# O's splits moved to block 1, VectorE's order in block 0's FFN changed, the overflow flag read earlier, and a tail whose down projection runs five steps back

## The chip, the cores and the metric

One core of a Trainium2 chip. The metric is the device time of one execution in microseconds (us). The kernel before takes 905.08 us (median of three runs, 904.69 to 905.27). The engines are named as in the profile: PE (TensorE, matmuls), PEld (its weight loads), DVE (VectorE), ACT (ScalarE), POOL (GpSimd) and SP (SyncE, which issues most DMAs).

## The reference, cut to what matters

x is 4 sequences of 1024 tokens with 512 features, in float32. A retention layer and a feed-forward network (FFN) stand each between two layer norms:

```python
x = x + _layernorm(attn(_layernorm(x)))      # attn, per token and feature:
#   q, v = x @ Wq.T, x @ Wv.T
#   ret[t] = lam * ret[t-1] + v[t]            (a scan along the sequence; 16 heads, one lam each)
#   out = layernorm(q * ret, gamma, beta) * silu(x @ Wg.T);  out @ Wo.T
x = x + _layernorm(ffn(_layernorm(x)))       # ffn:
#   silu(x @ fp8(gate_w) * gate_s) * (x @ fp8(up_w) * up_s) @ fp8(down_w) * down_s
```

The FFN is 512 to 1536 to 512, and its weights are rounded to 8-bit floats first.

## The kernel before, in words

**Blocks.** The 4096 tokens are NB = 8 blocks of TB = 512 tokens, each of NS = 4 sub-tiles of 128 tokens. The loop `for t in range(NB)` runs the FFN of block t in NI = 12 steps of 128 hidden features (`f.gate(i)`, `f.up(i)`, `f.fuse(i)`, `f.down(i - f.lag)`), and into its steps it weaves the retention layer of block t + 1 (object `b`), the first norm of block t + 2 (`n`) and the end of the FFN of block t − 1 (`l`). Block 0's retention layer, the splitting and rounding of weights, and block 1's v, q and g run ahead of the loop. `InOrder` keeps every engine's instructions in the order in which the code issues them; so an operation that waits holds up all behind it on its engine.

**Three passes.** From block FAST = 2 on (`fast`), and for block 1's v, q, g, a product in float32 is made of three passes on operands of fewer mantissa bits: top x top, low, and diff (`pass_of`, `o_pass`). `begin` makes the first two and then lets ACT scale the bank by 1 + LOW; `end` makes the diff pass and whatever reads the bank (scan for v, the product y for q with POOL's sum of y, SiLU for g). Activations are split by DVE: `cut_x` and `low_of` (an integer TENSOR_SCALAR, then a subtraction), `part_x` and `diff_of`.

**The splitter.** `Splitter` (line 323) does the same to weights. `units` numbers them: v is 0 to 3, q 4 to 7, g 8 to 11, o 12 to 15. `copy` ("c") copies a weight's chunk to DRAM, `split` ("s", line 365) is three DVE operations and one ACT scaling of 128x512, `store` ("k") writes parts to DRAM, and `keep` ("w") loads O's parts into `wo_parts`, which stays in SBUF. The table `times` (line 406) says at which block, step and place of the step O's are done, and `splitter.at(t, i, place)` does them. From block 2 on SP streams the parts of v, q, g and O's diff from DRAM into `w_ring`, four slots of 256 KB (`fetch_weights`).

**Rounding of the FFN's weights.** `round_weights` (line 175) takes 18 pieces; each is a DVE cast to 8 bits, a DMA of the next raw piece into the freed place, and an ACT copy back to SBUF, which also sums the piece into `over`. The generator yields three times a piece, and `rounds(n)` advances it n times. `pass_over` (line 200) makes one number of `over`: not zero if a weight overflowed. It writes a column of 128 numbers to DRAM, reads it back as a row, reduces it and writes `flag`. At the end every engine loads `flag`, and the program branches to a second, exact version if it isn't zero (label `beyond`).

**Block 0's FFN** (conditions `t == 0`) carries block 1's means and variances: `b.halves` splits a sum into two parts (ACT, then DVE), `b.mean` and `b.var` are two PE matmuls each with those parts, `center_y` subtracts, `z` scales and gates y, `o`, `o_moments`, `x1_of`, `x1n_of` finish the retention layer. It also carries block 2's first norm: `n.stats`, `rstd`, `shift`, `norm_x`, `send_x`, `low_of`, `diff_of`. Two PSUM banks with the tag `pf` serve gate and up in turn: gate's bank is freed by ACT's SiLU, up's by DVE's `fuse`.

**The tail** (from line 1493). In the last block the down projection lags by `self.lag` = 4 steps behind up, so 5 steps are left after the last up, done sub-tile by sub-tile. Then for each sub-tile DVE scales the bank (`scale`), makes statistics, ACT takes a root, DVE inverts it, the norm and the addition of x1 follow (`norm`, `add`), and a DMA writes `out`. The last sub-tile's addition is cut into two halves with a DMA each (`add_halves`).

Of the kernel before, what the change touches and what calls it, by code (L numbers as in the profile page):

```python
# [10 lines left out]
F32 = mybir.dt.float32  # L11
# [4 lines left out]
ALU = mybir.AluOpType  # L16

P = 128
# [5 lines left out]
def sandwich(  # L24
# [20 lines left out]
    nc = tc.nc  # L45
    NT, D = x.shape
# [3 lines left out]
    TB = 512  # L50
    NS = TB // P
    NB = NT // TB
# [7 lines left out]
    work = ctx.enter_context(tc.tile_pool(name="work", bufs=2))  # L60
# [6 lines left out]
    class InOrder:  # L67
# [9 lines left out]
    pe, dve, act, pool, sp = (  # L77
        InOrder(e) for e in (nc.tensor, nc.vector, nc.scalar, nc.gpsimd, nc.sync)
    )
# [116 lines left out]
    def rounds(n):  # L196
        for _ in range(n):
            next(rounding, None)
# [117 lines left out]
    operands = {}  # L316
# [4 lines left out]
    wo_parts = {}  # L321

    class Splitter:
# [40 lines left out]

        def split(self, n):
            k, c = units[n]
            if k == "o" and c == 0:
                w, top, low = wo_sb[:, c], self.room[0], self.room[1]
                diff = top
            elif k == "o" and c == 1:  # L370
                w = wo_sb[:, c]
                top = work.tile([P, D], F32, tag="rstd", name=f"top_o{c}", bufs=1)
                low = work.tile([P, D], F32, tag="ret", name=f"low_o{c}")
                diff = top
            elif k == "o":
                w, top = wo_parts["top"].bitcast(F32)[:, c], self.room[n % 2]
                low, diff = wo_parts["low"][:, c], top
            else:
                w, top = self.raw[k].bitcast(F32)[:, :, ts(c, P)], self.by_chunk(self.room[n % 2])
                low, diff = self.slot_of[k, c] = self.slots[len(self.slot_of) % len(self.slots)]  # L380
            dve.tensor_scalar(top.bitcast(I32), w.bitcast(I32), TOP_MASK, None, ALU.bitwise_and)
            dve.tensor_tensor(low, w, top, ALU.subtract)
            m = low.bitcast(F32)
            dve.scalar_tensor_tensor(diff, top, -LOW, m, ALU.mult, ALU.add)
            act.activation(low, m, AF.Copy, scale=1.0 / LOW)
            self.at_work[n] = {"diff": diff} if k == "o" and c > 1 else {"diff": diff, "low": low}

        def store(self, n):
            k, c = units[n]
# [11 lines left out]
        def keep(self, n):  # L401
            k, c = units[n]
            if c == 0:
                room = big.tile([P, 2, NC, D], F32R, tag="x1n0", name="wo_parts")
                wo_parts["top"], wo_parts["low"] = room[:, 0], room[:, 1]
            for part in ("top", "low"):
                if part in operands[k, c]:
                    sp.dma_start(wo_parts[part].bitcast(F32)[:, c], operands[k, c][part])

        times = {  # L410
# [4 lines left out]
        }  # L415

        def at(self, *when):
# [491 lines left out]
    class Ffn:  # L909
# [3 lines left out]
        def __init__(self, a):  # L913
            self.t, self.kept = a.t, a.kept
            self.parts = [a.x1nT[:, 0], a.x1nT[:, 1]]
            self.f, self.g = {}, {}
            self.last = self.t == NB - 1
            self.lag = 4 if self.last else 2
            self.x1, self.d = [], [None] * NS
            if self.last:  # L920
                self.more = [
                    big.tile([P, 2, 2, TB], F32R, tag=tag, name=f"more_{tag}") for tag in ("xnT", "y")
                ]
# [83 lines left out]
            center(self.d[s], self.d[s], self.mv[:, s, :])  # L1007

        def add(self, s, engine=pool):
            if engine is dve and s == NS - 1:  # L1010
                return self.add_halves(s)
            engine.tensor_tensor(self.d[s], self.d[s], self.x1[s], ALU.add)
            self.store(s)

        def add_halves(self, s):
            for h, queue in enumerate((sp, act)):
                cols = ts(h, D // 2)
                dve.tensor_tensor(self.d[s][:, cols], self.d[s][:, cols], self.x1[s][:, cols], ALU.add)
                queue.dma_start(out[ds(self.t * TB + s * P, P), cols], self.d[s][:, cols])

        def store(self, s):
            sp.dma_start(out[ds(self.t * TB + s * P, P), :], self.d[s])
# [11 lines left out]
    b = Retention(1)  # L1034
# [9 lines left out]
    a = Retention(0, x_first)  # L1044
    a.new_xnT()
    warm(14)
    early, later = slice(0, TB // Q // 2), slice(TB // Q // 2, TB // Q)
# [24 lines left out]
    wo_sb = load_square(woT, "wo_sb")  # L1072
# [27 lines left out]
    b.turn_x(1, "pd1")  # L1100
    a.v(3, "pf")
    a.scan(3)
    splitter.load("v")
    for n in range(2, 4):
        load_piece(n)
# [25 lines left out]
    a.var()  # L1131
    for s in range(NS):
        b.part_x(s)
    a.rstd_y()
    splitter.store(0)
    for c, home in enumerate(("pa0", "pf", "pf", "pa1")):
# [22 lines left out]
    a.o(2, "pd2")  # L1159
    rounds(3)  # L1160
    splitter.split(4)
    a.o_moments(2)
    a.x1_moments(1)
    a.x1_of(2)
    a.x1n_of(1)
    splitter.store(3)
    a.o(3, "pd3")
    a.new_x1nT()
    b.begin("v", 0, "pf")
    a.turn_x1n(0)  # L1170
    a.upper_of(0)
    a.o_moments(3)
    a.x1_moments(2)
    a.x1_of(3)
    a.x1n_of(2)
    a.rest_of(0)
    b.begin("v", 1, "pf")
    a.turn_x1n(1)
    a.upper_of(1)
    b.end("v", 0)  # L1180
    splitter.split(5)
    splitter.store(4)
    b.begin("v", 2, "pd0")
    a.rest_of(1)
    b.end("v", 1)
    a.turn_x1n(2)
    a.upper_of(2)
    b.begin("v", 3, "pd1")
    a.x1_moments(3)
    a.x1n_of(3)  # L1190
    a.rest_of(2)
    b.end("v", 2)
    splitter.split(6)
    splitter.store(5)
    b.begin("q", 0, "pd2")
    b.end("v", 3)
    b.begin("q", 1, "pd3")
    a.turn_x1n(3)
# [4 lines left out]
    a.rest_of(3)  # L1203
    b.begin("q", 2, "pf")
    b.end("q", 1)
    b.begin("q", 3, "pf")
    b.end("q", 2)
    rounds(3)
    b.end("q", 3)
    splitter.store(7)  # L1210
    rounds(3)

    l = None
    for t in range(NB):
        f, n = Ffn(a), None
        fast = b is not None and b.fast
        for i in range(NI):
            if t > 0 and (t > 1 or i) and not (fast and i == 11):
                (f if i else l).rest((i - 1) % NI)
            if t == 0 and i == 0:  # L1220
                n = Retention(2)

            if t > 0 and b and i == 0 and t < NB - 2:
                n = Retention(t + 2)
# [17 lines left out]
            if fast and i == 3:  # L1242
                l.stats(3)
                l.rstd()
                l.shift()
            if t == 0 and i == 4:
                b.z(0)
            if t == 0 and 7 <= i < 10:
                b.x1_moments(i - 7)
            f.gate(i)  # L1250
            if t == 0 and i in (5, 6):
                n.norm_x(2 * i - 10, True)
                n.norm_x(2 * i - 9, True)
# [22 lines left out]
            if fast and i == 6:  # L1276
                b.gate_y(3)
                b.cut_y(3)
            if t == 0 and i == 1:
                b.halves()  # L1280
            if t == 0 and i == 3:
                b.var()
            if t == 0 and i == 4:
                b.z(1)
            if t == 0 and i == 5:
                b.z(2)
                b.z(3)
            if t == 0 and 6 <= i < 10:
                b.o(i - 6)
            if t == 0 and i == 8:  # L1290
# [26 lines left out]
            if t == 0 and i == 1:  # L1317
                b.mean()
                b.center_y()
            if t == 0 and i == 2:  # L1320
                b.halves()
            if t == 0 and i == 9:
                load = b.move_x1n(2)
                load()
# [12 lines left out]
            if fast and i == 11:  # L1337
                for s in range(2):
                    b.upper_of(s)
                    b.rest_of(s)  # L1340
            if t == 0 and i == 3:
                b.rstd_y()
            if fast and i == 4:
                b.halves()
            if fast and i < 6:
# [23 lines left out]
            if fast and i == 7:  # L1369
                b.rest_of_y()  # L1370
            splitter.at(t, i, "mid")
            if t == NB - 1 and 1 < i < 5:
                next(passing, None)
            if n and t and i == 2:
                l.fetch(0, 2)
# [17 lines left out]
                    n.diff_of(2)  # L1393
                    n.diff_of(3)
            if t == 0:
                rounds(3 if 0 < i < 6 else 6 if i < 8 else 0)
                if i < 11:
                    f.rest(i)
                if 0 < i < 5:
                    n.stats(i - 1)  # L1400
                if i == 4:
                    n.rstd()
                    n.shift()
                if i == 8:
                    n.low_of(0)
                    n.low_of(1)
                if i in (9, 10):
                    n.low_of(i - 7)

            if l and not b and i in (4, 5):  # L1410
                l.stats(2 * i - 8)
# [91 lines left out]
    for s in range(2, NS):  # L1503
        for i in steps:
            l.down(i, [s])
    beyond = None
    if flag is not None:
        loads, (beyond,) = nc.values_load_multi_w_load_instructions(
            flag, min_val=0, max_val=0x7F800000,
            skip_runtime_bounds_check_because="it is compared with zero alone",  # L1510
        )
        for load in loads:
            tc.keep_in_program_order(load)
        tc.mark_branch_hint_location("beyond", beyond, engines=mybir.ALL_ENGINES)
    for s in range(NS):
        l.scale(s)
        l.stats(s)
        l.root(s)
        if s:
            l.add(s - 1, dve)  # L1520
        l.inverse(s)
        l.norm(s, shift_scale if s < NS - 1 else center_scale)
    l.add(NS - 1, dve)
    return beyond


# [92 lines left out]
```

## Time and profile before

| | |
|---|---|
| median of the runs | 905.08 us |
| the profiled execution | 904.03 us |
| its span | 902.2 us |
| instructions | 12010 |
| busy: PE, DVE, ACT, POOL | 881.1, 629.8, 419.0, 238.9 us |
| O splits on DVE, start | 148.91, 158.64, 197.31, 199.75 us |
| first gate matmul of block 0, of block 1 | 104.44, 192.87 us |
| last matmul's end | 892.65 us |
| landing of the last output | 900.01 us |

The profile is of one execution, whose own time stands in the table beside its span; sums over its rows are compared with it, and not with the median. All operations are issued through one helper line (L75), so groups are told apart by the tiles that they write and read: `pfg` and `pfu` are the banks of gate and up, `pd` that of down, `pv`, `pq`, `pg` those of v, q, g, `po` that of O; `mu` and `var` those of block 1's mean and variance; `half` the parts of a sum, `ysum` and `sqsum` POOL's sums; `split_room` and `wo_parts` the O splits; `scr` the rounding pieces. A row of waits says which engine's work on which tile ended the wait of another engine's instruction. The matmuls' listed durations overlap, so the distance of their starts is of more use than their lengths.

### The profile page before, as it was taken

The numbers are of one execution on the slowest core, as the hardware profiler recorded it, in microseconds if no ns is written. First come the engines' busy times: TensorE is split into PE (matmuls) and PEld (weight loads), VectorE is DVE, ScalarE is ACT, GpSimd is POOL, SyncE is SP. The second block draws the span as 40 slices with busy tenths as digits, with TensorE's granted clock in tenths as the row PEclk, the third lists the DMA queues.
The fourth block names the chain that finished last, engine by engine and source line by source line (L and its number), as shares of the span: only waits on it lengthen the run. The fifth ranks groups of instructions, "written<-read, shape, count | busy, mean of one in ns | idle before, by whom it ended". The sixth has DMA issues, their size and how long they took to land. (4 is left out here: it accounts for less than half of the span.)

```text
span 902.2 us, 12010 instructions
## 1 busy us (share of the span) xinstructions
PE 881.1 (98%) x3948; PEld 738.6 (82%) x3948; DVE 629.8 (70%) x1071; ACT 419.0 (46%) x741; POOL 238.9 (26%) x304
## 2 busy tenths in 40 slices
PE   9999999889999999999999999999999999999995
PEld 7465777678888888888888888888888888888885
DVE  4898788677587766876668675876758756665545
ACT  1358566533645336453464435553364523644323
POOL 1215212201415024230423214141232403322020
PEclk9999999999999999999999999999999999999998
DMA  9974444767563674646754766728746565424021
GB/s 284 304 217 157 151 171 157 205 234 237 171 176 96 232 237 136 153 153 204 250 149 97 232 205 193 187 58 258 226 148 152 154 197 149 152 73 117 0 94 50
DMA packets 116154, 153.73 MB, mean 170 GB/s; under 512 B 10931, under 2 KB 54708, under 8 KB 116020
## 3 DMA queue, kind: packets, MB, share of 16 engines
q1 hardware_dynamic: 115220, 152.23, 55.1%
q8 instruction: 33, 0.54, 0.2%
q10 hardware_dynamic: 864, 0.66, 0.2%
q14 instruction: 37, 0.30, 0.1%
HBM read 117.98 MB, written 39.06 MB: 174 GB/s over the span
## 5 line engine op out<-in xcount | busy, mean ns | idle before, releaser
L75 PE MATMUL pfg<-x1nT,gate_sb 128*128 128x512 f32 x768 | 182.8, 381 | 3.3 <-ACT gate L75 3.2
L75 PE MATMUL pfu<-x1nT,up_sb 128*128 128x512 f32 x768 | 183.2, 381 | 0.8 <-DVE gate L75 0.8
L75 PE MATMUL pd<-down_sb,fuse 128*128 128x512 f32 x720 | 170.5, 379 | 0.0
L75 PEld LDWEIGHTS pfg<-x1nT,gate_sb 128*128 128x128 f32 x768 | 144.2, 189 | 26.7 <-ACT gate L75 6.2
L75 PEld LDWEIGHTS pfu<-x1nT,up_sb 128*128 128x128 f32 x768 | 145.0, 189 | 23.6 <-issue 1.7
L75 PEld LDWEIGHTS pd<-down_sb,fuse 128*128 128x128 f32 x720 | 141.4, 197 | 14.5
L75 DVE SCALAR_TENSOR_TENSOR gate<-pfu,us_sb,gate 128x512 f32<-128x512 f32 x96 | 71.8, 747 | 67.0 <-PE pfu L75 54.8
L75 ACT CAST fuse<-gate 128x512 fp32r<-128x512 f32 x90 | 55.6, 617 | 126.9 <-DVE gate L75 125.2
L75 ACT ACTIVATE gate<-pfg,gs_sb 128x512 f32<-128x512 f32 x96 | 65.6, 683 | 95.5 <-PE pfg L75 95.4
L75 POOL TENSOR_SCALAR mv<-mv 128x1 f32<-128x1 f32 (+1 forms) x82 | 22.8, 278 | 315.0 <-DVE mv L75 312.9
L75 DVE TENSOR_TENSOR fuse<-gate,fuse 128x512 fp32r<-128x512 f32 x90 | 71.7, 797 | 7.4 <-ACT fuse L75 7.3
L75 POOL TENSOR_TENSOR d<-d,x 128x512 f32<-128x512 f32 x28 | 41.7, 1510 | 84.5 <-ACT d L75 70.6
L75 DVE BATCH_NORM_STATS2 st<-x 128x6 f32<-128x512 f32 x64 | 43.6, 681 | 15.2 <-POOL x L75 12.5
L75 POOL TENSOR_TENSOR mv<-mv,nhalf 128x1 f32<-128x1 f32 (+1 forms) x75 | 51.8, 691 | 6.2
L75 POOL TENSOR_TENSOR x<-x,x1n 128x512 f32<-128x512 f32 x32 | 44.7, 1403 | 23.4 <-ACT x1n L75 15.0
L75 ACT ACTIVATE pv<-pv 128x512 f32<-128x512 f32 x28 | 16.3, 581 | 52.9 <-PE pv L75 52.9
L75 POOL TENSOR_TENSOR sqsum<-sqsum,sq 128x512 f32<-128x512 f32 x24 | 33.6, 1401 | 16.0 <-ACT sq L75 8.7
L75 POOL TENSOR_TENSOR ysum<-y 128x512 f32<-128x512 f32 x8 | 10.2, 1275 | 104.2 <-DVE y L75 104.2
L75 DVE TENSOR_TENSOR y<-pq,y 128x512 f32<-128x512 f32 x28 | 19.1, 682 | 22.5 <-PE pq L75 22.5
L75 DVE SCALAR_TENSOR_TENSOR y<-y,lnb_sb,mids 128x512 f32<-128x512 f32 x28 | 27.0, 965 | 7.1 <-ACT mids L75 7.0
L75 ACT ACT_TABLE_LOAD x19 | 24.4, 1283 | 15.5 <-DVE var L75 11.1
L75 DVE BATCH_NORM_STATS2 st<-po 128x6 f32<-128x512 f32 x32 | 21.9, 683 | 13.4 <-PE po L75 13.4
(222 smaller groups left out, 1482.8 us busy)
## 6 DMA issues: line engine op xcount, KB each, us to landing
x<-in_x SPq DMA_DIRECT2D x52, 256.0 KB, 5.6
kept<-x SPq DMA_DIRECT2D x32, 256.0 KB, 2.9
x<-kept SPq DMA_DIRECT2D x32, 256.0 KB, 4.4
out<-d SPq DMA_DIRECT2D x31, 256.0 KB, 2.0
w_ring<-dtop_v SPq DMA_DIRECT2D x24, 256.0 KB, 4.1
w_ring<-dlow_v SPq DMA_DIRECT2D x24, 256.0 KB, 3.2
w_ring<-ddiff_v SPq DMA_DIRECT2D x24, 256.0 KB, 3.6
w_ring<-dtop_q SPq DMA_DIRECT2D x24, 256.0 KB, 2.6
```

The lines of the kernel that those rows point to most:

```text
L75: return lambda *args, **kwargs: tc.keep_in_program_order(op(*args, **kwargs))
```

## The change

1. **O's splits.** `split` treats all four chunks of O alike: the source is `wo_parts["top"]` (loaded at block 0's last step), the low part stays in `wo_parts`, and only diff is written to DRAM. `keep` loads top alone. The splits of O's chunks 0 and 1 leave block 0, and all four stand at the start of steps 2, 3, 4 and 5 of block 1.
2. **Ahead of the FFN.** Two `rounds(3)` are added, one behind `a.scan(3)` and one ahead of `a.rstd_y()`; others are spread differently. `a.o(3)` and block 1's v passes begin earlier, and the transposes and moments around them are reordered.
3. **Block 0's FFN.** `b.halves` comes ahead of `f.up`, `b.var` behind `f.fuse(3)`; the statistics of block 2's input come in two pairs (steps 2 and 3); `z` and `rstd_y` are placed differently; `n.low_of` comes up to a step earlier; the rounding's steps per FFN step change.
4. **The flag.** `pass_over` moves from block 7 to block 3, steps 0 to 2. ACT, SP and POOL also load the flag and get a branch hint in block 6, step 5; at the end all five engines load it, and only DVE and PE get the hint there.
5. **The tail.** `self.lag` is 5 in the last block, so 6 steps of down are left after the last up, 12 matmuls for each sub-tile instead of 10. The last sub-tile is centered ahead of its reciprocal, and then scaled and added in two halves of 256 columns, each one DVE operation and a DMA.

The diff's core:

```diff
-            if k == "o" and c == 0:
-                w, top, low = wo_sb[:, c], self.room[0], self.room[1]
...
+            if k == "o":
                 w, top = wo_parts["top"].bitcast(F32)[:, c], self.room[n % 2]
                 low, diff = wo_parts["low"][:, c], top
...
-            self.at_work[n] = {"diff": diff} if k == "o" and c > 1 else {"diff": diff, "low": low}
+            self.at_work[n] = {"diff": diff} if k == "o" else {"diff": diff, "low": low}
...
-            for part in ("top", "low"):
-                if part in operands[k, c]:
-                    sp.dma_start(wo_parts[part].bitcast(F32)[:, c], operands[k, c][part])
+            sp.dma_start(wo_parts["top"].bitcast(F32)[:, c], operands[k, c]["top"])
...
-            (0, 6, "end"): "s12", (0, 7, "start"): "k12", (0, 7, "end"): "s13", (0, 8, "start"): "k13",
-            (0, 11, "mid"): "w12 w13 w14 w15", (1, 0, "start"): "r s14", (1, 0, "mid"): "s15",
-            (1, 0, "end"): "k14", (1, 1, "start"): "k15",
+            (0, 11, "mid"): "w12 w13 w14 w15", (1, 2, "start"): "r s12", (1, 3, "start"): "k12 s13",
+            (1, 4, "start"): "k13 s14", (1, 5, "start"): "k14 s15", (1, 5, "end"): "k15",
...
-            self.lag = 4 if self.last else 2
+            self.lag = 5 if self.last else 2
...
+        def center(self, s):
+            dve.tensor_scalar(self.d[s], self.d[s], self.mv[:, s, 0:1], None, ALU.subtract)
+
+        def spread(self, s):
+
             for h, queue in enumerate((sp, act)):
                 cols = ts(h, D // 2)
-                dve.tensor_tensor(self.d[s][:, cols], self.d[s][:, cols], self.x1[s][:, cols], ALU.add)
-                queue.dma_start(out[ds(self.t * TB + s * P, P), cols], self.d[s][:, cols])
+                d = self.d[s][:, cols]
+                dve.scalar_tensor_tensor(
+                    d, d, self.mv[:, s, 1:2], self.x1[s][:, cols], ALU.mult, ALU.add
+                )
+                queue.dma_start(out[ds(self.t * TB + s * P, P), cols], d)
...
     a.scan(3)
+    rounds(3)
...
         b.part_x(s)
+    rounds(3)
     a.rstd_y()
...
     splitter.split(4)
+    a.o(3, "pd3")
+    b.begin("v", 0, "pf")
     a.o_moments(2)
...
+            if t == 0 and i == 3:
+                b.halves()
+                n.stats(2)
+                n.stats(3)
+                n.rstd()
+                n.shift()
...
+                for k in {8: (0, 1), 9: (2,)}.get(i, ()):
+                    n.low_of(k)
             f.gate(i)
+            if t == 0 and i == 1:
+                b.halves()
+            if t == 0 and 0 < i < 8 and i != 4:
+                rounds(2)
...
-            if t == 0 and i == 1:
-                b.halves()
-            if t == 0 and i == 3:
-                b.var()
...
-            if t == 0 and i == 2:
-                b.halves()
+            if t == 0 and i == 3:
+                b.var()
+            if t == 0 and i == 10:
+                n.low_of(3)
...
-            if t == NB - 1 and 1 < i < 5:
+            if flag is not None and t == NB - 2 and i == 5:
+                hint(load_flag(early), early)
+            if t == 3 and i < 3:
                 next(passing, None)
...
-                rounds(3 if 0 < i < 6 else 6 if i < 8 else 0)
+                rounds({0: 4, 3: 0, 6: 4, 7: 3}.get(i, 1 if i < 7 else 0))
                 if i < 11:
                     f.rest(i)
-                if 0 < i < 5:
-                    n.stats(i - 1)
-                if i == 4:
-                    n.rstd()
-                    n.shift()
-                if i == 8:
-                    n.low_of(0)
-                    n.low_of(1)
-                if i in (9, 10):
-                    n.low_of(i - 7)
+                if i == 2:
+                    n.stats(0)
+                    n.stats(1)
+                if i == 3:
+                    b.rstd_y()
...
         if s:
             l.add(s - 1, dve)
+        if s == final:
+            l.center(s)
         l.inverse(s)
-        l.norm(s, shift_scale if s < NS - 1 else center_scale)
-    l.add(NS - 1, dve)
+        if s < final:
+            l.norm(s, shift_scale)
+    l.spread(final)
```

More of the change, by code (lines that the diff above doesn't have):

```diff
@@ L366, in split @@
             k, c = units[n]
-            if k == "o" and c == 0:
-                w, top, low = wo_sb[:, c], self.room[0], self.room[1]
[L369 to L375, printed above, removed]
+            if k == "o":
                 w, top = wo_parts["top"].bitcast(F32)[:, c], self.room[n % 2]
@@ L1009, in add @@
         def add(self, s, engine=pool):
-            if engine is dve and s == NS - 1:
-                return self.add_halves(s)
             engine.tensor_tensor(self.d[s], self.d[s], self.x1[s], ALU.add)
             self.store(s)
-        def add_halves(self, s):
+        def center(self, s):
+            dve.tensor_scalar(self.d[s], self.d[s], self.mv[:, s, 0:1], None, ALU.subtract)
+        def spread(self, s):
             for h, queue in enumerate((sp, act)):
                 cols = ts(h, D // 2)
-                dve.tensor_tensor(self.d[s][:, cols], self.d[s][:, cols], self.x1[s][:, cols], ALU.add)
-                queue.dma_start(out[ds(self.t * TB + s * P, P), cols], self.d[s][:, cols])
+                d = self.d[s][:, cols]
[3 more added lines that the diff above has]
+                queue.dma_start(out[ds(self.t * TB + s * P, P), cols], d)
         def store(self, s):
@@ L1164, in sandwich @@
     a.x1_of(2)
+    b.begin("v", 1, "pf")
     a.x1n_of(1)
     splitter.store(3)
-    a.o(3, "pd3")
     a.new_x1nT()
-    b.begin("v", 0, "pf")
     a.turn_x1n(0)
@@ L1174, in sandwich @@
     a.x1_of(3)
+    b.end("v", 0)
+    b.begin("v", 2, "pd0")
     a.x1n_of(2)
     a.rest_of(0)
-    b.begin("v", 1, "pf")
+    b.end("v", 1)
     a.turn_x1n(1)
     a.upper_of(1)
-    b.end("v", 0)
     splitter.split(5)
     splitter.store(4)
-    b.begin("v", 2, "pd0")
     a.rest_of(1)
-    b.end("v", 1)
+    b.begin("v", 3, "pd1")
+    b.end("v", 2)
     a.turn_x1n(2)
     a.upper_of(2)
-    b.begin("v", 3, "pd1")
     a.x1_moments(3)
     a.x1n_of(3)
+    b.begin("q", 0, "pd2")
     a.rest_of(2)
-    b.end("v", 2)
     splitter.split(6)
     splitter.store(5)
-    b.begin("q", 0, "pd2")
     b.end("v", 3)
@@ L1205, in sandwich @@
     b.end("q", 1)
+    rounds(1)
     b.begin("q", 3, "pf")
     b.end("q", 2)
-    rounds(3)
+    rounds(2)
     b.end("q", 3)
@@ L1211, in sandwich, with load_flag, hint @@
     rounds(3)
+    late = [mybir.EngineType.DVE, mybir.EngineType.PE]
+    early = [mybir.EngineType.Activation, mybir.EngineType.SP, mybir.EngineType.Pool]
+    def load_flag(engines):
+        loads, (value,) = nc.values_load_multi_w_load_instructions(
+            flag, engines, min_val=0, max_val=0x7F800000,
+            skip_runtime_bounds_check_because="it is compared with zero alone",
+        )
+        for load in loads:
+            tc.keep_in_program_order(load)
+        return value
+    def hint(value, engines):
+        tc.mark_branch_hint_location("beyond", value, engines=engines)
     l = None
@@ L1249, in sandwich @@
                 b.x1_moments(i - 7)
+                for k in {8: (0, 1), 9: (2,)}.get(i, ()):
+                    n.low_of(k)
             f.gate(i)
+            if t == 0 and i == 1:
+                b.halves()
+            if t == 0 and 0 < i < 8 and i != 4:
+                rounds(2)
             if t == 0 and i in (5, 6):
@@ L1278, in sandwich @@
                 b.cut_y(3)
-            if t == 0 and i == 1:
-                b.halves()
-            if t == 0 and i == 3:
-                b.var()
[L1283 to L1287, printed above, removed]
             if t == 0 and 6 <= i < 10:
@@ L1319, in sandwich @@
                 b.center_y()
-            if t == 0 and i == 2:
-                b.halves()
+            if t == 0 and i == 3:
+                b.var()
+            if t == 0 and i == 10:
+                n.low_of(3)
+            if t == 0 and i == 4:
+                b.z(1)
+                b.z(2)
+            if t == 0 and i == 5:
+                b.z(3)
             if t == 0 and i == 9:
@@ L1340, in sandwich @@
                     b.rest_of(s)
-            if t == 0 and i == 3:
-                b.rstd_y()
             if fast and i == 4:
@@ L1505, in sandwich @@
             l.down(i, [s])
-    beyond = None
+    beyond = load_flag(late + early) if flag is not None else None
     if flag is not None:
[L1508 to L1514, printed above, removed]
+        hint(beyond, late)
+    final = NS - 1
     for s in range(NS):
```

## The prediction

> **What bounds the kernel now.** I read the page's busy times first, then the engines' busy time stage by stage, then what TensorE (PE) waited for in the stages that are not full.
>
> ```profile
> PE 881.1 (98%) x3948; PEld 738.6 (82%) x3948; DVE 629.8 (70%) x1071; ACT 419.0 (46%) x741; POOL 238.9 (26%) x304
> ...
> 80.00:104.00 24.00, 22.12 (x107) 18.21 (x107) 18.90 (x37) 14.40 (x30) 7.51 (x13) 1.00 0.41 135
> 104.00:136.00 32.00, 29.08 (x127) 23.21 (x126) 25.48 (x40) 21.23 (x36) 7.70 (x5) 1.00 0.56 190
> 136.00:170.00 34.00, 34.00 (x128) 24.05 (x127) 24.35 (x42) 20.45 (x41) 9.51 (x16) 1.00 0.63 185
> 170.00:192.00 22.00, 17.41 (x80) 14.49 (x79) 16.96 (x30) 8.68 (x17) 5.43 (x8) 1.00 0.49 159
> 192.00:240.00 48.00, 47.41 (x215) 40.29 (x214) 34.41 (x61) 19.57 (x32) 13.11 (x16) 1.00 0.75 245
> 240.00:560.00 320.00, 319.94 (x1486) 279.40 (x1484) 228.40 (x388) 150.67 (x264) 93.50 (x115) 1.00 0.60 179
> ```
>
> In each window the first figure after its length is PE's busy time. From 240 us to the tail PE is full at granted clock 1.00: nothing but fewer matmuls helps there, and the change removes none. What can be won is PE's idle time in block 0 and at the start of block 1, and the tail after the last matmul (ends 892.65; span 902.2).
>
> The seen idle understates a stall. Back to back, eight 128x512 matmuls start 1.72 apart (0.2155 each) but are listed at 0.38, so 0.165 of a stall lies under the listed end, and the restart costs about 0.1 more. By start-to-start distance over 0.2155 the stalls are: **A**, 82–104 us, 3.0; **B**, 104–136, 4.8; **C**, 170–190, 5.4; **D**, 198–223, 1.4; under 1 afterwards. The waits name them (two answers, B's window and then C's and D's):
>
> ```profile
> PE mu L75 <- ACT half L75: 1.0, 1, 1.0
> PE pfg L75 <- ACT gate L75: 0.9, 2, 0.6
> ...
> PE pfg L75 <- ACT gate L75: 2.3, 1, 2.3
> PE pv L75 <- DVE low L75: 1.5, 1, 1.5
> PE pfu L75 <- DVE gate L75: 0.8, 1, 0.8
> PE pv L75 <- DMA w_ring<-dtop_v: 0.2, 1, 0.2
> ```
>
> **C: two O splits leave the end of block 0.** Each split is TENSOR_SCALAR 0.42, TENSOR_TENSOR 0.69, SCALAR_TENSOR_TENSOR 0.69 on DVE, 1.8 with what lies between. The two of block 0 hold DVE at 148.91–151.82 and 158.64–160.5, 4.8 together, ahead of everything that fills the end of the block; DVE's casts end late, so gate 9 frees its bank late (pfu 0.81), SiLU 10 follows (pfg 2.29), and low_of reaches the v pass late (1.49). Without 4.2 of this and with low_of called a step earlier I walked the chain again: gate 9 done near 168 against PE's need at 171; SiLU 10 near 172 against 174.4; low_of(3) near 174.7 against 178.8; the last diff 180.5 against 181.8. The smallest slack is 1.3, so all three stalls go: **5.4** (4.0 if the last piece stays late).
>
> **B: halves ahead of f.up, statistics bundled, rounding later.** The mean's stall is 1.76 with the pfg before it 0.59. DVE's half needs ACT's half first, and ACT's waits behind two rounding copies (1.06 + 0.19 each). With halves earlier and the rounding after SiLU about 1.0 of the 2.35 stays; the pfg at 120.18 (0.85) goes; the var stall (1.37) stays and grows a little, to 1.8, because two statistics (0.68 + 0.18 each) now stand ahead of the lower half on DVE; 0.24 at 132.6 goes. 1.35 + 0.85 − 0.4 + 0.24 = 2.04, say **2.1** (1.0–3.5).
>
> **A: order ahead of the FFN, two rounding pieces earlier.** o(3) and the v passes begin sooner, so the pv end (1.18) and pq (0.66) mostly go; pt(3) now waits some 1.45 for x1n_3, against 0.85, as split 5 goes ahead of its moments. One added cast (0.68) lies in DVE's gap at 37–39.6, the other delays rstd_y's chain by 0.65 where DVE has slack later. Sum **0.95** (0–2).
>
> **D: SP moves less.** Two of six w DMAs of 256 KB (about 0.66 us apart on the queue) no longer stand ahead of w_ring, and four stores of block 0 are gone: the stalls at 198.3 and 202.4 go, **0.8** (0.3–1.0); pq's at 222.75 is counted below.
>
> **What it costs: four splits in steps 2–5 of block 1, where PE now hardly waits.** The place of the first:
>
> ```profile
> 219.40 0.68 DVE L75 TENSOR_TENSOR y<-pq,y 128x512 f32<-128x512 f32 x1
> 220.00 0.68 DVE L75 BATCH_NORM_STATS2 st<-d 128x6 f32<-128x512 f32 x1
> ...
> 220.81 0.74 DVE L75 SCALAR_TENSOR_TENSOR gate<-pfu,us_sb,gate 128x512 f32<-128x512 f32 x1
> ```
>
> ```profile
> 220.16 1.28 POOL L75 TENSOR_TENSOR ysum<-y 128x512 f32<-128x512 f32 x1 [10.50 <-DVE y L75]
> ```
>
> ```profile
> 221.59 0.62 ACT L75 CAST fuse<-gate 128x512 fp32r<-128x512 f32 x1 [4.43 <-DVE gate L75]
> 222.11 0.58 ACT L75 ACTIVATE pq<-pq 128x512 f32<-128x512 f32 x1
> ```
>
> Split 12 falls between y and gate; ACT's cast waits for gate, the pq scale is queued behind the cast, and PE's diff pass already waits for it (0.53 at 222.75). So the 1.8 go straight to PE, and 2.8 if POOL's add of the same y stretches the split. How it stretches, from block 0:
>
> ```profile
> 149.33 0.69 DVE L75 TENSOR_TENSOR split_room<-wo_sb,split_room 128x512 f32<-128x512 f32 x1
> 150.06 1.76 DVE L75 SCALAR_TENSOR_TENSOR split_room<-split_room 128x512 f32<-128x512 f32 x1
> ```
>
> ```profile
> 150.01 1.27 POOL L75 TENSOR_TENSOR x<-x,x1n 128x512 f32<-128x512 f32 x1 [4.43 <-ACT x1n L75]
> ```
>
> Over the whole trace, of the DVE TENSOR_TENSORs to fp32r that start inside a POOL operation 23 of 30 take longer, mean 1.30, against 0.68 for the 178 others; integer TENSOR_SCALARs 16 of 16, mean 1.11 against 0.44. [...]
>
> Split 13, between y at 228.30 and gate at 230.03 (a gap of 1.03 before it): half, then mu at 233.21, late by 0.2, or 1.3 with POOL's add at 229.35–230.63. Split 14, after the fuse rest at 236.56: half at 240.59 and var at 241.73 late by 0.7, or 2.6 under POOL's square sums (236.25–240.55). Split 15 lies in DVE's gap of 2.10 before the gate at 248.64: 0. Together **2.7** with no stretching, 6.7 with it. The nearest rows stretch, so I take **6.7**; with every one a little worse 7.2.
>
> **pass_over in block 3, flag loads in block 6.** Some 0.5 of DVE, beside a full PE; DVE's rest in block 7 (3.43 for the row) is free already. The column's DMA took 6.8 from issue to landing; SP reaches the row's DMA about 11 after it, so nothing behind waits. Loads of the flag took 0.64 (ACT) to 1.46 (SP) at the tail; in block 6 they stand in queues with slack: 0 (up to 0.5). The hints at the end are under the last output's landing (900.01): 0. [...]
>
> **The tail.**
>
> ```profile
> 892.99 0.67 DVE L75 TENSOR_TENSOR d<-d,x 128x512 f32<-128x512 f32 x1
> 893.58 0.15 DVE L75 RECIPROCAL mvd<-mvd 128x1 f32<-128x1 f32 x1
> 893.65 0.67 DVE L75 TENSOR_TENSOR d<-pd,ds_sb 128x512 f32<-128x512 f32 x1
> ```
>
> DVE needs about 2.4 for a sub-tile; PE delivers one in 10 matmuls, 2.155, so DVE is behind by 1.0 at the last (893.65 against 892.65). With 12 matmuls, 2.59, it keeps up: the last scale starts 0.1 after PE. Two SCALAR_TENSOR_TENSORs of 256 columns (about 0.48, estimated from 0.74 for 512 and 0.42 for an add of 256) take the place of two adds; center no longer waits for the reciprocal. **0.95** (0.7–1.1).
>
> **The sum**, against the profiled execution's 904.03: gains 5.4 + 2.1 + 0.95 + 0.8 + 0.95 = 10.2 (6 to 13), cost 6.7 (2.7–7.7): −3.5, 900.5. The median of the runs (905.08) is 1.05 above the profiled execution: **901.5**. About 0.2% (1.8 us) is what a measurement tells from no change: faster is below 903.3, slower above 906.9.
>
> **Rivals.**
> 1. The splits are not stretched: POOL's adds start after them, or a shifted order passes them by. Cost 2.7: 905.08 − 10.2 + 2.7 = **897.6**. For it: 7 of 30 TENSOR_TENSORs escape, and with C gone block 1 starts 8 us earlier against the same DMAs. Against: the split follows the very y that POOL adds.
> 2. The change doesn't do what it says: DVE's 17 us of casts and statistics are reordered and the stalls move to another wait (pt(3) in A, var in B), which leaves C 4.0, D and the tail, 5.7, against 6.7 of cost: about **905**, same. For it: A and B are 72–80% full on DVE, and one late operation delays all behind it.
> 3. Slower: in steps 2–5 of block 1 every split is stretched in all its three operations (1.11 + 1.30 + 1.30 = 3.7), and ACT's scaling of the low part (0.63), queued ahead of pq, pg and half, adds to each: 4 × 4.3 − 3.1 (gaps at 230.03 and 248.64) = 14.2: **909**. It decides from a cost of 12.0 on (10.2 + 1.8). For it: ACT is in order and the pq scale is its next entry; against: DVE's gaps there, and POOL's adds cover one or two operations, not three.
>
> **Numbers.** Forecast 0.53, rival 1 0.18, rival 2 0.17, rival 3 0.12. Faster: 0.52 + 0.18 = 0.70; same 0.01 + 0.17 = 0.18; slower 0.12. The range leaves out rival 3 and the far end of rival 1 (gains 13 with cost 2.7, 894.8): 896.0 to 906.0.
>
> **What would show it.** C: no PE wait over 0.3 in the last two steps of block 0, and block 1's first pfg near 184.4 instead of 192.87. B: a var wait of about 1.0 seen, no pfg wait. D: no wait for w_ring. Block 1: waits for ACT pq of about 2.5 near the second q pass, at mu about 1 and at var about 2, split operations over 1 us beside POOL's adds. Tail: the last scale within 0.2 of PE's end. A wait for pv or pfg left at the end of block 0, or none in block 1, makes it wrong.

## The result, and the profile after

The changed kernel takes 908.65 us (median of 17 runs, 904.92 to 911.21) against 905.72 for the kernel before (17 runs, of which the 905.08 above is the median of the first three): ratio 1.0032, 95% interval 1.0025 to 1.0039. It is slower by 2.9 us, where 3.5 of gain were forecast; the time lies outside the range. Its profiled execution took 907.72, its span is 905.9 (902.2 before).

The same stages as before, with PE's busy time first in each window:

```profile
PE 883.4 (98%) x3948; PEld 741.3 (82%) x3948; DVE 631.2 (70%) x1071; ACT 418.5 (46%) x741; POOL 239.0 (26%) x304
...
80.00:104.00 24.00, 22.56 (x110) 18.56 (x109) 20.03 (x39) 15.20 (x33) 8.46 (x14) 1.00 0.46 156
104.00:136.00 32.00, 30.39 (x137) 25.61 (x136) 27.59 (x43) 20.95 (x34) 8.89 (x9) 1.00 0.52 177
170.00:192.00 22.00, 21.26 (x100) 18.25 (x100) 15.15 (x27) 8.59 (x17) 3.42 (x5) 1.00 0.69 223
192.00:240.00 48.00, 43.25 (x189) 36.63 (x187) 35.75 (x56) 18.24 (x30) 14.01 (x16) 0.96 0.61 194
240.00:560.00 320.00, 315.56 (x1451) 274.17 (x1452) 227.83 (x392) 147.28 (x259) 88.84 (x112) 0.99 0.61 176
```

The holes of block 0 have shrunk (0.7 of 22 us idle at its end, 4.6 before), and new ones have opened: 4.8 in the stage of block 1, and 4.4 in the long stage that had been full. In both the granted clock, the figure after POOL's, is below 1.00.

What PE waited for, from the stage ahead of the FFN to the tail (total, times, longest):

```profile
PE pq L75 <- DMA w_ring<-dtop_q: 2.9, 1, 2.9
PE pq L75 <- ACT pq L75: 2.7, 2, 2.6
PE var L75 <- ACT half L75: 1.9, 1, 1.9
```

These are the three largest rows. The second and third were forecast. The first, at 420.8 to 423.75 us in block 3, was not. Of the signs set down for the end of block 0, one failed: a wait of 0.5 for `pfg` is left there, and block 1's first gate matmul stands at 185.52, not near 184.4.

To place every loss, I matched the matmuls of the two traces by order and took the difference of their starts (after less before; negative is ahead). The first column names the tile written and the matmul's start in the kernel before; a stage's gain or loss is the step from the row above:

| up to | difference | what lies there |
|---|---|---|
| first transposes (11 us) | −0.38 | start, differs between executions |
| pq at 97 us | −1.09 | A |
| pfu at 134 us | −3.15 | B |
| pv diff at 190 us | −7.34 | C |
| pv at 202 us | −8.23 | D |
| pg at 242 us | −0.58 | block 1, +7.65 |
| pq at 329 us | −0.39 | block 2 |
| pq at 435 us | +4.70 | block 3, +5.09 |
| last matmul's end | +5.13 | blocks 4 to 7 |
| last VectorE operation's end | +4.18 | tail, −0.95 |

The span ends 3.7 later. So the kernel was 8.2 us ahead at the start of block 1, had lost nearly all of it by block 2, and lost 5 more in block 3.

**Block 1.** The changed kernel's DVE, POOL, ACT and PE around split 12, one fence for each:

```profile
210.65 0.68 DVE L75 TENSOR_TENSOR y<-pq,y 128x512 f32<-128x512 f32 x1
211.25 0.41 DVE L75 TENSOR_SCALAR split_room<-wo_parts 128x512 int32<-128x512 int32 x1
211.70 1.64 DVE L75 TENSOR_TENSOR wo_parts<-wo_parts,split_room 128x512 fp32r<-128x512 f32 x1
```

```profile
211.41 1.38 POOL L75 TENSOR_TENSOR ysum<-y 128x512 f32<-128x512 f32 x1 [9.59 <-DVE y L75]
```

```profile
214.10 0.63 ACT L75 ACTIVATE wo_parts<-wo_parts 128x512 fp32r<-128x512 f32 x1 [5.24 <-DVE split_room L75]
215.57 0.62 ACT L75 CAST fuse<-gate 128x512 fp32r<-128x512 f32 x1 [0.84 <-DVE gate L75]
216.09 0.58 ACT L75 ACTIVATE pq<-pq 128x512 f32<-128x512 f32 x1
```

```profile
216.72 2.06 PE L75 MATMUL pq<-diff,w_ring 128*128 128x512 f32 x4 [2.55 <-ACT pq L75]
218.58 1.83 PE L75 MATMUL pq<-xnT,w_ring 128*128 128x512 f32 x4
```

The chain is the one forecast: the subtraction that starts inside POOL's add takes 1.64 instead of 0.69 and ends 0.55 after the add does, then gate, cast, the pq scale, PE. What the forecast lacked is in the last two lines: the four matmuls of a pass are listed at 1.83 to 2.06 instead of 1.03. PE runs at half pace (0.427 from start to start instead of 0.2155) while the granted clock is 0.50, in this case for the 3.41 us from 216.78 on.

**Block 3.** SP's DMAs in the changed kernel, and then the wait:

```profile
412.62 0.38 SPq L75 DMA_DIRECT2D beyond<-total  x1
414.80 0.32 SPq L75 DMA_DIRECT2D w_ring<-dtop_q  x1
```

```profile
423.75 1.10 PE L75 MATMUL pq<-xnT,w_ring 128*128 128x512 f32 x4 [2.94 <-DMA w_ring<-dtop_q]
```

The column's write, issued at 412.62, landed at 420.95; the load of w_ring issued 2.2 after it landed at 423.62, 8.8 after its issue. The issue rows of the changed kernel, of the kernel before's whole page (24 such loads) and of its block 7, one fence for each; the last figure is the median from issue to landing:

```profile
w_ring<-dtop_q SPq DMA_DIRECT2D x1, 256.0 KB, 8.8
```

```profile
w_ring<-dtop_q SPq DMA_DIRECT2D x24, 256.0 KB, 2.6
```

```profile
beyond<-total SPq DMA_DIRECT2D x1, 0.5 KB, 6.8
```

The DMA view of the changed kernel from 414 to 419 us, in forty slices (busy tenths, then GB/s; a packet counts in the slice in which it begins):

```profile
DMA  8866221000000099000000000000000000027991
GB/s 328 295 214 85 82 82 17 0 0 0 0 0 0 0 164 98 0 0 0 0 0 0 0 0 0 0 0 0 0 0 0 0 0 0 33 82 164 147 33 66
```

For more than two microseconds no packet begins, though three loads are queued: the sixteen packets of 2 KB that began from 415.75 to 415.99 took 2.6 to 6.7 us, 4.06 on average. In the kernel before the same write stood in block 7, where no load follows it.

### The profile page after: what moved, and what is told of

It reads as the page before. It is cut to its first block, busy times and chain, and to the rows that moved or that the text cites. A ratio compares the mean times of both kernels' runs of the same rounds, so it can differ in the third digit from the quotient of the medians.

```text
span 905.9 us, 11996 instructions
## 1 busy us (share of the span) xinstructions
PE 883.4 (98%) x3948; PEld 741.3 (82%) x3948; DVE 631.2 (70%) x1071; ACT 418.5 (46%) x741; POOL 239.0 (26%) x304
## 4 chain that ended last, share of the span: by engine, by line
PE 84%; DVE 7%; DMA 4%; ACT 2%; issue 2%; POOL 1%; SPq 0%; DVEq 0%; ACTq 0%; POOLq 0%
PE pfg L75 16%; PE pd L75 16%; PE pfu L75 16%; PE pg L75 9%; PE po L75 9%; PE pv L75 8%; PE pq L75 8%; DVE y L75 2%; DMA mx<-xs 1%; DVE st L75 1%; DMA w_ring<-dtop_q 1%; DVE gate L75 1%; PE idle L75 1%; ACT x1n L75 1%; DMA x<-in_x 1%
## 5 line engine op out<-in xcount | busy, mean ns | idle before, releaser
L75 ACT ACTIVATE pq<-pq 128x512 f32<-128x512 f32 x28 | 16.2, 580 | 32.6 <-PE pq L75 32.6
```

The costliest lines, as they stand in the source:

```text
L75: return lambda *args, **kwargs: tc.keep_in_program_order(op(*args, **kwargs))
```

## The experiments

Theory Q: the 128 numbers of 4 bytes that `pass_over` writes in block 3 hold the DMAs behind them. Theory S: block 1 loses by the splits and by the lower clock behind their stalls. The rivals: all the loss is in block 1 (B), and block 1 loses because PE comes too early, whatever the splits do (W).

**p7**: pass_over back in block 7, all loads of the flag at the end.

```diff
-            if flag is not None and t == NB - 2 and i == 5:
-                hint(load_flag(early), early)
-            if t == 3 and i < 3:
+            if t == NB - 1 and 1 < i < 5:
...
-        hint(beyond, late)
+        hint(beyond, late + early)
```

> The changed kernel with pass_over back in block 7 and without the early flag loads and hints. Theory Q (the 128 writes of 4 bytes in block 3 hold w_ring's loads behind them, 3.1 us of PE waiting and some 2 us more at half pace): the wait for w_ring at block 3 is gone, PE's shift against the kernel before stays near -0.5 us until the tail, and the time is 903 to 904 (ratio 0.997 to 0.998). Rival B (block 1's splits make the loss and block 3 is only where it shows): 907 to 909, ratio 1.002 to 1.004.

Measured 906.98, ratio 1.0003 (0.9993 to 1.0013): between the two, outside both ranges. The wait of block 3 is gone as Q says. But PE now waits 0.9 in block 7 for VectorE's product (1.05 with the restart), which neither foresaw, and the profiled execution had two stretches of half pace in block 1 instead of one (clock 0.65 from 220 to 224 us and 0.66 from 244 to 248), so that PE was 2.4 behind after it, not 0.5 ahead.

**col_act**: the column from ACT's queue.

```diff
-        sp.dma_start(column, bits)
+        act.dma_start(column, bits)
```

> The changed kernel with the column written by a DMA of ACT's queue instead of SP's. If the column holds only the DMAs behind it on SP's queue, w_ring's loads in block 3 land in 2.6 us as elsewhere and the time is 903 to 904.5. If the column holds the DMA engines whatever queue it is from, the stall of about 3 us stays and the time is 907 to 909.

Measured 908.18, ratio 1.0029 (1.0015 to 1.0043). The column took 8.9 to land, the load of w_ring issued by SP 2.4 after it 9.3, and PE waited 1.9 and 1.2 for w_ring. So it isn't SP's queue that is held, but what the two queues share; whether that is the DMA engines or the memory behind them, no run tells.

**col_apart**: the numbers 512 bytes apart, still 4 bytes each.

```diff
-        column = dram.tile([P, 1], I32, tag="beyond", name="beyond", bufs=1)
+        column = dram.tile([P, P], I32, tag="beyond", name="beyond", bufs=1)[:, 0:1]
```

> The changed kernel with the column's 128 numbers written 512 bytes apart in DRAM, still 4 bytes each. If the writes are slow because they all fall into one stretch of 512 bytes, the DMA lands in under 4 us and the time is 903 to 904.5. If writes of 4 bytes are slow as such, it takes 6 to 9 us as before and the time is 907 to 909.

Measured 904.22, ratio 0.9981 (0.9971 to 0.9991): faster than before, 4.4 less than the changed kernel. The column landed after 3.35, the load behind it after 2.6, and no wait for w_ring is left. p7's median lies 2.8 above this one: 1.05 of that is its wait in block 7, and its profiled execution had one stretch of half pace more, 1.7; whether the medians differ by the same is not shown.

**col_512**: 512 bytes for each partition.

```diff
-        column = dram.tile([P, 1], I32, tag="beyond", name="beyond", bufs=1)
-        sp.dma_start(column, bits)
+        wide = work.tile([P, TB], I32, tag="ret", name="wide")[:, :P]
+        dve.tensor_copy(wide, bits.to_broadcast([P, P]))
+        square = dram.tile([P, P], I32, tag="beyond", name="beyond", bufs=1)
+        sp.dma_start(square, wide)
+        column = square[:, 0:1]
```

> The changed kernel with 512 bytes written for each of the 128 partitions (the number repeated), of which the row reads one each; DVE makes one operation of 128x128 more. If writes under 512 bytes are what holds the queue, the write lands in under 3.5 us, w_ring's loads come in time and the time is 903 to 904.5. If any write to DRAM ahead of w_ring's loads holds them, the stall stays, 907 to 909.

Measured 904.62, ratio 0.9988 (0.9977 to 0.9999); the write landed after 4.3, not under 3.5, but the load behind it after 2.7, and no wait for w_ring is left. So neither the number of writes nor their 4 bytes holds the DMAs by itself, but that all 128 lie side by side, within 512 bytes (the load behind: 8.8 in the changed kernel, 2.6 in col_apart, 2.7 here). How far apart is enough, no run shows: 512 bytes is the only other distance tried. The DMA view of 414 to 419 us in col_apart, beside the one above:

```profile
GB/s 213 246 213 180 246 328 263 246 214 165 83 50 49 33 33 16 0 0 82 213 131 98 180 246 360 426 279 262 246 311 246 344 279 295 246 213 246 295 295 377
```

Why writes side by side hold the DMAs, no run shows; at the distance of col_apart, 4 bytes each held nothing.

**apart_early**: col_apart with O's splits where DVE had been seen idle and POOL without work.

```diff
-            (0, 11, "mid"): "w12 w13 w14 w15", (1, 2, "start"): "r s12", (1, 3, "start"): "k12 s13",
-            (1, 4, "start"): "k13 s14", (1, 5, "start"): "k14 s15", (1, 5, "end"): "k15",
+            (0, 11, "mid"): "w12 w13 w14 w15", (1, 0, "mid"): "r s12 s13", (1, 0, "end"): "k12",
+            (1, 1, "mid"): "k13 s14", (1, 2, "mid"): "k14", (1, 5, "start"): "s15", (1, 5, "end"): "k15",
```

> The changed kernel with the column's numbers 512 bytes apart, and O's splits at other places of block 1: 12 and 13 behind step 0's product of gate and up, 14 behind step 1's, 15 where the change has it. There VectorE is idle for 3.6 and 1.9 us in the changed kernel's profile, and POOL has nothing to do. Theory S (block 1's loss of 7.6 us is the splits' 1.8 us each on VectorE, POOL's stretching, ACT's low part, and the lower clock after PE's stalls): PE's waits for ACT pq, mu and var in block 1 fall to those of the kernel before (0.5, 0.3, 0.3), no half pace follows, and the time is 896.5 to 899 (ratio 0.990 to 0.992). Rival W (block 1 loses because PE comes 8 us earlier than the data of block 1's y, whatever the splits do): the waits stay above 2 us and the time is 902 to 905.

Measured 897.22, ratio 0.9912 (0.9897 to 0.9926), as S says. Of the waits in block 1's stage one row is left:

```profile
PE pq L75 <- ACT pq L75: 1.1, 2, 0.8
```

and no stretch of half pace (mean clock 0.997, that of the kernel before); this wait is longer than the 0.5 expected, those at mu and var are gone. None of the four splits is stretched any more: their operations take at most 0.42, 0.70 and 0.70. From 202 to 262 us block 1 loses 1.1 instead of 7.65. W falls: PE comes 7.1 us early here too.

**o_alone**: the kernel before with the first item of the change alone (`split`, `keep` and the table `times`).

> The kernel before with O's splits moved as the change moves them, and nothing else. Gain by the prediction: most of the end of block 0 (4 to 5.4 us) and SP's loads (0.8); cost 6 to 8 in block 1, and 1.5 to 3.5 where the clock drops behind a stall. Together 906 to 910, slower than before. If the move pays for itself: 900 to 904.

Measured 913.24, ratio 1.0081 (1.0068 to 1.0094): worse than expected. Its PE is 1.0 us ahead at the end of block 0, not 4 to 5, and it loses 9.8 in block 1. Three stalls, one in block 0 and two in block 1, are followed by six to nine matmuls at half pace (the mean clock of the profiled execution is 0.992); without the first of these stretches, 1.6 long, it would be some 2.5 ahead. In its stage of 170 to 192 us PE still waits:

```profile
PE pfg L75 <- ACT gate L75: 2.2, 1, 2.2
```

**order_alone**: the kernel before with the second and third items alone.

> The kernel before with the new order ahead of the FFN and in block 0's FFN alone (O's splits, pass_over, the flag and the tail as before). By the prediction's A and B 3.0 us of gain, and some of the end of block 0 (low_of earlier): 901.5 to 903.5. If the order only moves the stalls: 905 to 907.

Measured 900.35, ratio 0.9938 (0.9925 to 0.9951): better than expected. PE is 2.8 us ahead at 134 us and 5.8 ahead at the v pass of the table's row C, with both O splits still in block 0.

**tail_alone**: the kernel before with the fifth item alone.

> The kernel before with the new tail alone (lag 5, center and spread). Gain 0.95 by the prediction: 904.5 to 905.2 (ratio 0.9988 to 0.9994). If the tail's end is set by the last transfer whatever VectorE does: 905.9, ratio 1.000.

Measured 905.77, ratio 1.0002 (0.9994 to 1.0011). This doesn't show that the tail gains nothing: PE waits in block 7 as in p7.

```profile
PE pfu L75 <- DVE gate L75: 1.3, 1, 1.3
```

There DVE stands 4.14 for pass_over's row. With a lag of 5 the eight matmuls of down that covered this in the kernel before (3.43 for the row, no wait of PE) come a step later.

**tail_apart**: tail_alone with pass_over in block 3, 512 bytes apart, and the early flag loads.

> The kernel before with the new tail, and pass_over in block 3 with the column 512 bytes apart, the early flag loads and the hints. In the tail alone PE waited 1.4 us in block 7 for a product that VectorE held back while it waited for pass_over's row; that wait has no place here: 904.3 to 905.0 against 905.6. If the tail gains nothing of itself: 905.4 to 906.

Measured 903.58, ratio 0.9976 (0.9965 to 0.9987); no wait in block 7 is left. The gain of 2.0 is above the 0.6 to 1.3 expected; where the rest comes from is open.

**apart_before**: col_apart with the splitter of the kernel before (two splits in block 0, two at block 1's start).

> The changed kernel with the column 512 bytes apart and O's splits where the kernel before has them (two in block 0, two at the start of block 1). The new order alone took 5.2 us off with the splits in block 0, so little of the end of block 0 is owed to moving them: 898.5 to 900 (order 5.2 and tail 1.0 to 1.2 off 905.6), at most 2 us over the 897.2 of the splits in block 1's gaps. If the splits in block 0 cost the 4 us that the prediction put down to them, 901 to 903.

Measured 898.75, ratio 0.9926 (0.9913 to 0.994), as expected. Against apart_early two splits in block 0 cost some 1.5 us by the medians, though the intervals overlap; by the traces the pfg stall at the end of block 0 is 1.9 with restart, where the changed kernel has 0.7.

**reordered**: apart_early with two orders of VectorE changed.

```diff
+    a.x1_moments(3)
     splitter.split(5)
...
-    a.x1_moments(3)
...
                 b.halves()
-                n.stats(2)
-                n.stats(3)
+                for k in range(NS):
+                    n.stats(k)
...
-                if i == 2:
-                    n.stats(0)
-                    n.stats(1)
```

> As the kernel with the column apart and the splits in block 1's gaps (897.2), with two of VectorE's orders changed for what is waited for: the four statistics of block 2's input stand behind the lower half of the square sum (PE waits 1.5 at var for that half), and the moments of the last sub-tile's x1 ahead of split 5 (PE waits 1.3 at a transpose for them). Both waits go: 894.6 to 895.5. If the work put behind is late in their place, 896.5 to 898.

Measured 896.80, ratio 0.9900 (0.9885 to 0.9916). Both waits are gone, but others stand in their place (1.1 for ACT's pv, 0.5 for the low part of a split, 0.6 for a pfg at 129 us): the miss is on the side of "put behind is late". It is the fastest kernel of the study, by less than the intervals can tell from apart_early.

## Why the prediction was wrong, by its own steps

**The step that failed** is the one on pass_over: "The column's DMA took 6.8 from issue to landing; SP reaches the row's DMA about 11 after it, so nothing behind waits." The term stood in the sum at 0 (up to 0.5). It asked only who needs the column. The transfers of w_ring issued behind it are held with it, from whichever of the two queues the column is written, and in block 7, where the 6.8 was read, there are none. Measured: 5.1 in block 3, of which 3.1 are the wait, 1.7 half pace behind it and 0.2 a later wait. Putting the numbers apart brings 4.4 back. That the write might hold the ring's DMAs was given no price. An estimate could be had from two rows of the kernel before: a load that must wait until the column has landed comes some 4 us late (6.8 less 2.6).

**What was missing altogether** is the granted clock. I priced a stall at its length and the restart. The clock view of the changed kernel and of col_apart around block 1's first stall:

```profile
212.00:216.00 4.00, 2.17 (x11) 1.61 (x9) 3.93 (x6) 1.06 (x2) 0.79 (x1) 1.00 0.90 315
216.00:220.00 4.00, 3.27 (x8) 2.65 (x9) 1.43 (x4) 0.67 (x2) 0.27 (x1) 0.60 0.14 32
```

```profile
216.00:220.00 4.00, 3.02 (x14) 2.67 (x15) 2.32 (x6) 0.99 (x3) 0.94 (x1) 1.00 0.25 89
```

In the first PE makes 8 matmuls in four microseconds at a clock of 0.60; in the second, after a stall of like length (2.9 waited, 2.6 in the first), 14 at 1.00. Half pace makes up 1.7 of block 1's loss and 1.7 of block 3's.

**Block 1's cost**, 6.7 forecast, was 7.65: the waits 2.2 (q), 1.2 (mu) and 2.5 (var), 6.0 together, against 2.8, 1.3 and 2.6, and 1.7 of half pace. The mechanism and the places were right, the fourth split was free as forecast, and the rival without stretching is refuted by the rows above. Rival 3's sign came, and its 909 lies near the measured 908.65, but by luck: no split was stretched in all three operations, and of its cost of 14.2 in block 1 only 7.65 came. The reading behind rival 1, that 7 of 30 operations escape, was too hopeful: five of the seven began inside a POOL operation of about 1.0 us on one column, and of the 25 that began inside one of 512 columns 23 were stretched (25 of 28 in the changed kernel). Rival 2's sum, 5.7 against 6.7, is about 905 from the profiled execution, but 906 from the median that rivals 1 and 3 use.

**C**, 5.4 forecast, came to 4.2, but for another reason than I gave. I put it down to the two splits that leave block 0. The order alone, with the splits in place, brought 3.1, and the splits on top of it about 1 (moved alone, some 2.5 but for a stretch of half pace). The chain had been walked once, with all edits in it, and the credit given to the largest.

**A** 0.95 forecast, 0.7 measured; **B** 2.1 and 2.1; **D** 0.8 and 0.9; **the tail** 0.95 and 0.95 (from PE's last end to DVE's: 4.66 before, 3.71 after). These steps held. Of the early loads and hints I found no trace in the times, and no run tried them alone.

**The sum**: −3.5 forecast, +3.7 in the profile, 7.2 apart: 5.1 for block 3, 1.0 for block 1 above the forecast, 1.2 for C are 7.3; the rest is within what two executions differ by.

## What to carry to other kernels

- Price a DMA that is moved by what is queued behind and beside it at the new place, not only by who waits for its result; a latency read where the queues are empty says nothing of a place where loads stream (here 6.8 in block 7, 8.3 in block 3, and the load behind it 8.8 instead of 2.6).
- On a full TensorE a new stall of two microseconds can cost more than two: allow for 1.7 more of half pace behind it (it came behind 12 of 18 here), and read the granted clock stage by stage (0.96 in block 1's stage of the changed kernel), not its mean (0.995).
- VectorE work that must move goes where a trace shows VectorE idle and GpSimd without work; block 1 lost 7.65 us with the four splits in one place, and 1.1 with three of them two to three steps earlier.

## What the runs showed of the hardware that I had not expected

**Small writes to one place.** 128 writes of 4 bytes side by side took 6.8 us to land in the kernel before, 8.3 in the changed kernel and 8.9 from ACT's queue in col_act; the loads of w_ring behind the last two took 8.8 and 9.3. 512 bytes apart, in col_apart, the writes took 3.35 and the load behind them 2.6, as elsewhere.

**The clock.** In the profiles of this study 18 stalls of PE of 2.0 to 3.4 us (with restart) stand in blocks 0 to 3. Behind 12 of them PE made at least six matmuls at half pace, 1.3 to 1.8 us lost each time; behind 6 it didn't, among them one of 3.17 in col_512. Behind shorter stalls, apart_before's of 1.9 among them, it was not seen.

The granted clock falls to 0.50 for 3.413 us at a time: in the changed kernel from 216.776 and from 424.989 us, behind waits of PE of 2.55 and 2.94. These two begin 208.213 us apart, 61 times 3.413; the two in block 1 begin 23.89 apart, 7 times 3.413, in col_act, p7 and o_alone.

What parts the 12 stalls from the 6 is left open; their length alone does not. At the q pass of block 1 PE waited 2.4 in col_act and 3.2 in p7 with half pace behind it (clock 0.78 and 0.65 from 220 to 224 us), and 2.9 in col_apart and 3.0 in col_512 without (1.00). At block 1's var a stall of 2.06 was followed by it in p7 (clock 0.66 from 244 to 248 us), and one of 2.06 in the changed kernel was not (1.00). So the place in the code doesn't decide it either, and a forecast can give it only a chance. The time goes with it: the changed kernel's 17 runs spread over 6.3 us, from 904.92 at a mean clock of 0.997 to 911.21 at 0.992, and p7's twelve from 903.8 at 0.998 to 908.2 at 0.993.
